# A two-level Strassen MLP: the output bias, S1's sums, A12's own sums and two sets of weight sums put elsewhere

## The chip, the cores and the metric

The kernel runs on one core of a Trainium2 chip. A core has five engines that run their own instruction streams: TensorE (PE; its weight loads are listed as PEld) multiplies matrices, VectorE (DVE), ScalarE (ACT) and GpSimd (POOL) work element by element, and SyncE (SP) issues the DMA transfers here. They are held together by semaphores. Each engine takes its instructions in program order, so an instruction that waits holds up everything behind it on that engine. The metric is the device time of one execution in microseconds; the median of three runs is compared.

## The reference

A cross-attention block and an MLP in float32, with 8 batches of 256 query tokens and 256 context tokens, a model width of 512 and an inner width of 2048. Cut to what matters here:

```python
hidden = cproj(attention(layer_norm(x), ctx)) + x
y = layer_norm(hidden, ln2_w, ln2_b)
y = gelu(y @ fc_w + fc_b, approximate=True)
y = y @ proj_w + proj_b
return hidden + y
```

The change lies in the last three lines, the MLP.

## The kernel before

**Stages.** The first part (to about 350 us) computes the attention for all four groups of 512 tokens and leaves `hidden` in DRAM. The MLP then runs group after group, g = 0 to 3. For each group the first product of the MLP (`fc`, 512 to 2048) comes first, then gelu, then the second product (`proj`, 2048 to 512).

**Strassen's method in Winograd's form.** A product of two matrices, each cut in 2 x 2 blocks, is made of seven block products instead of eight, with sums of blocks taken beforehand and sums of the results afterwards. The blocks of the left matrix A are summed to S1, S2, S3, S4, those of the right matrix B to T1, T2, T4, and the seven products are A11 B11, A12 B21, S2 T2, S3 B12, S1 T1, S4 B22 and A22 T4. In the kernel the sums of A are named `s1` to `s4` and those of B `t1`, `t2`, `t4`. The tables `A_SUMS` and `B_SUMS` hold the four sums of each side.

**`fc`.** `product(k, ...)`, k = 0 to 6, is one of the seven products, and is itself cut into seven by `sub`. One `sub` has eight matmul records. Its results go to PSUM banks (tile `pf`), and VectorE adds them into `u` and then into `h` or `hs`; where a product counts in several blocks of the result, GpSimd adds `hs` into the others (`made`, on GpSimd at line 1122 as `h<-h,hs`). Banks 6 and 7 are single, banks 1 and 5 double. At its end `product` calls `load_w2`, which puts the load of a later product's weights into the ring place just read. The lists `gelus` and `norm` hold work of ScalarE and VectorE that `product` hands out.

**`proj`.** The sums S3 and S2 of the gelu's output are made first (`sum_h`; on VectorE in groups 1 to 3, which are called deep; on GpSimd in group 0), each in four pieces. Here `bias_ht` is called: it adds the output's bias to two quarters of the output tile `ht` (named `resm`), two GpSimd instructions. Then `proj` multiplies A11 by B11 and S3 by B12 whole. In the deep groups the products A12 B21, S2 T2, S1 T1 and S4 B22 are each cut into seven once more by `deep_proj`, which needs the left operand's own sums (`h_blocks`, four sums on VectorE) and the right operand's. VectorE adds each partial product from its bank into a scratch (`p<-pd,p`) and into the result. The instructions handed to `deep_proj` as `others` are put between these adds, in VectorE's order. A12's own sums go to the four quarters of `h["s3"]` (tile `hs`, `free(i)`), which the product S3 B12 still reads; its first two are made before `deep_proj`, the other two and the four sums of S1 are given as `others`. The last of these products, A22 T4, is again whole and accumulates into bank 7.

**Sums of the `proj` weights.** The right operands' own sums are made once by `p2_sums` (four sums of 128x512, then a store of 768 KB to DRAM on SP's queue), in a tile `p2` (shown as `p`) that has two places: `t2` and `22` share the first, `t1` and `21` the second. `t1`'s are made at the end of group 0. Those of `22` and `21` are made on GpSimd when group 1 begins, those of `t2` on VectorE, one in each of group 1's products 3 to 6. Later uses reload them with `p2_load`.

**The end of a group.** `turn_next` transposes the next group's input on TensorE, `sum_up` and `split_y` make its sums on VectorE (`y<-y`), and the last eviction of bank 7 (`o_add` at the very end of the group's loop, `resm<-py,resm`) is behind them in VectorE's order. Group 3 has no next group.

The order is written out by hand: the pools reuse tiles with waits, and there is no scheduler.

Of the kernel before, what the change touches and what calls it, by code (L numbers as in the profile page):

```python
# [22 lines left out]
def tile_xattn_block(  # L23
# [52 lines left out]
    NG = B // GB  # L76
# [9 lines left out]
    HI, HC, HF, HD2 = INNER // 2, NC // 2, NF // 2, D // 2  # L86
# [57 lines left out]
    def place(name, at):  # L144

        return Operand(wts.tile([P, 7, HC, S], F32, tag=f"w{at}", name=name))
# [23 lines left out]
    def rows_of(t):  # L170
        return t.rearrange("p i h s -> p i (h s)")
# [13 lines left out]
    w2, w2_place = {}, {}  # L185
# [137 lines left out]
    with ExitStack() as att:  # L323
# [460 lines left out]
        V, GP = nc.vector, nc.gpsimd  # L784
# [175 lines left out]
        g = 1  # L960
        begin(g, 6, 1, load_res, 0, *QUARTERS)
        begin(g, 7, 1, bias_res, 0)
        g = 2
# [6 lines left out]
        g = NG - 1  # L970
# [24 lines left out]
        def run(pieces):  # L995
            for p in pieces:
                p()
# [18 lines left out]
        t = work.tile([P, NHG, G], F32, tag="att", name="w2_b")  # L1016
# [84 lines left out]
    with ExitStack() as mlp:  # L1101
# [8 lines left out]
        NQF = HF // 2  # L1110
# [59 lines left out]
        def p2_sums(n, eng=V):  # L1170
            x = pw_blocks(n)
            for i in range(4):
                sum_up(eng, x, B_SUMS, i)
                if i == 3:
                    nc.sync.dma_start(p2_dram[n], p2_place(n))
                yield

        p2_t2 = p2_sums("t2")

        def p2_load(n):  # L1180
            nc.sync.dma_start(p2_place(n), p2_dram[n])
# [8 lines left out]
        for g in range(NG):  # L1190
# [18 lines left out]
            def sum_h(which, q, eng=GP):  # L1209

                x = {n: h[n][:, :, 2 * q : 2 * q + 2, :] for n in h}
                to, a, b, op = {
                    "s3": ("s3", "11", "21", ALU.subtract),
                    "s2": ("21", "22", "s3", ALU.subtract),
                    "s1": ("11", "21", "11", ALU.add),
                    "s4": ("12", "12", "21", ALU.subtract),
                }[which]
                add(eng, x[to], x[a], x[b], op)
# [21 lines left out]
            def bias_ht():  # L1240

                for b, bias in ((0, projb[:, :HD2]), (1, pbd)):
                    o = out_quarter(b, 0)
                    add(GP, o, o, by_tiles(bias))
# [8 lines left out]
            def gelu(n, half):  # L1253
                def one(p):
                    nc.scalar.activation(  # L1255
                        h[n][:, :, p, :],
                        h[n][:, :, p, :],
                        AF.Gelu_apprx_tanh,
                        bias=col(c_fcb, half * HF + p),
                        scale=1.0,  # L1260
                    )

                gelus.extend(lambda p=p: one(p) for p in range(HF))
# [5 lines left out]
            def product(k, *sums):  # L1269


                wt, yn = w2[g, k], QI[FC_ORDER[k][1]]
                bank = {}

                def y_of(n):
                    if n in QUARTERS:
                        return ys[g].t[:, yn, int(n[0]) - 1, ts(int(n[1]) - 1, P)]
                    return y2s[g][:, ("t1", "t2", "t4").index(n), yn, :]

                def sub(n, w, b, first, last):  # L1280
                    if first:
                        bank[n] = bank_of(n, f"pf{n}_{k}").rearrange("p i (j s) -> p (i j) s", j=2)
                    for m in range(HF // 2):
                        mm(
                            bank[n][:, m, :],
                            wt[:, QI[w], ts(m, P)],
                            y_of(b),
                            first and m == 0,
                            last,
                        )  # L1290

                def u(n):
                    return us(n, f"u{n}_{k}").rearrange("p i (j s) -> p (i j) s", j=2)

                def made(cd, n, x):
                    some_gelus()
                    if k in (3, 4) and cd != "22":
                        norm_piece()
                    if sums[0][1] is None:
                        add(V, block(sums[0][0], cd), bank[n], x)  # L1300
                        return

                    r = h["s3"][:, parts[0] % 4 // 2, parts[0] % 2 * HF // 2 :][:, : HF // 2]
                    parts[0] += 1
                    add(V, r, bank[n], x)
                    for to, base in sums:
                        add(GP, block(to, cd), block(base, cd), r)

                sub(1, "11", "11", True, False)
                u1 = u(1)  # L1310
                nc.scalar.copy(u1, bank[1])  # L1311
                if g == 1 and k > 2:
                    next(p2_t2)
                sub(6, "s2", "t2", True, True)
                u2 = u(2)
                add(V, u2, bank[6], u1)
                some_gelus()
                sub(7, "s3", "12", True, False)
                u3 = u(3)
                add(V, u3, bank[7], u2)  # L1320
                some_gelus()
                sub(5, "21", "t1", True, False)
                made("22", 5, u3)
                sub(1, "12", "21", False, True)
                some_gelus()
                for to, base in sums:
                    if base:
                        add(V, block(to, "11"), bank[1], block(base, "11"))
                    else:
                        nc.scalar.copy(block(to, "11"), bank[1])  # L1330
                sub(7, "22", "t4", False, True)
                made("21", 7, u2)
                sub(5, "s4", "22", False, True)
                made("12", 5, u2)
                load_w2(w2_place[g, k])


            if g == 1:
                for n in ("22", "21"):
                    for _ in p2_sums(n, GP):  # L1340
                        pass
            product(0, ("21", None))
            load_next()
            product(1, ("11", "21"))
            gelu("11", 0)
            ht = residual(work, hid_dram[g], "resm", f"resm_{g}")
            product(2, ("21", "21"))
            product(3, ("12", "21"))
            if g == 0:
                load_pw("11", "12", "22")  # L1350
# [15 lines left out]
            for which in ("s3", "s2"):  # L1366
                for q in range(NQF):
                    sum_h(which, q, V if deep else GP)
            bias_ht()

            bank = {n: bank_of(n, f"py{n}") for n in ((1, 7) if deep else (1, 7, 6, 5))}

# [20 lines left out]
            def turn_next(c):  # L1393
                if g + 1 < NG:
                    ps = ps_m.tile([P, G], F32, tag="mm", name=f"pyt_{g + 1}_{c}")
                    turn_hid(ps, g + 1, c)

            def o_add(eng, b, k, x):
                o = out_quarter(b, k)
                add(eng, o, x, o)  # L1400
# [13 lines left out]
            def free(i):  # L1414

                return h["s3"][:, i // 2, i % 2 * HF // 2 :][:, : HF // 2]

            def h_blocks(n, s3, s2, s4, s1=None):


                x = {
                    f"{i + 1}{k + 1}": h[n][:, i, k * HF // 2 : (k + 1) * HF // 2, :]
                    for i in range(2)
                    for k in range(2)
                }
                x |= {"s3": s3, "s2": s2, "s4": s4, "s1": x["21"] if s1 is None else s1}

                def one(to, a, b, op):
                    add(V, x["s1" if to == "21" else to], x[a], x[b], op)

                return x, [lambda t=t: one(*t) for t in A_SUMS]
# [33 lines left out]
            def as_tiles(r):  # L1465

                return r.rearrange("p c s -> p (c s)").rearrange("p (i s) -> p i s", i=2)

            if deep:
                x_s2, pieces = h_blocks("21", *(hsum[:, i] for i in range(4)))  # L1470
                run(pieces)
                s1_sums = [lambda q=q: sum_h("s1", q, V) for q in range(NQF)]
            else:
                for q in range(NQF):
                    sum_h("s1", q)
            proj(bank[7], "s3", "12", True, False)
            turn_next(0)
            turn_next(1)
            some_pw(4)
            if deep:  # L1480
                x_12, pieces = h_blocks("12", *(free(i) for i in range(4)))
                run(pieces[:2])
                deep_proj(
                    x_12, "21", hsum[:, 4], pieces[2:3], pieces[3:], s1_sums[:1], s1_sums[1:3], s1_sums[3:]
                )
                p2_load("t1")
                x_s1, s1_own = h_blocks("11", free(0), free(1), free(2))
                run(s1_own[:2])
            else:
                proj(bank[1], "12", "21", False, True)  # L1490
                o_add(V, 0, 0, bank[1])
            for q in range(NQF):
                sum_h("s4", q)
            if deep:
                o_add(GP, 0, 0, as_tiles(hsum[:, 4]))
            turn_next(2)
            turn_next(3)
            some_pw(4)
# [103 lines left out]
```

## Time and profile before

| what | value |
|---|---|
| median of 3 runs | 733.42 us (729.81 to 734.86) |
| the profiled execution | 734.46 us |
| its span | 732.70 us |
| mean granted TensorE clock | 0.998 |
| DMA over the span | 149.90 MB, 205 GB/s mean |
| group 0's MLP, `fc` and `proj` | 350.4 to 444.7 us |
| group 1 | 444.7 to 541.5 us |
| group 2 | 541.5 to 634.8 us |
| group 3 | 634.8 to the end |

The profile is one execution. A row of the timeline has the start and the duration in us, the engine, the line, the operation, what it writes and reads, the shape, and how many instructions were merged; in brackets is the idle time before it and whose end it waited for. A row of the list of waits has the total, the number and the longest. Helpers such as `add` (line 1122) and `sum_up` (line 219) record every operation under their own line, so tiles tell more than lines. The ends of matmuls are modelled, so rows of TensorE overlap a little; starts are used for differences.

### The profile page before, as it was taken

The page shows a single profiled execution, that of the slowest core. Times are in us where ns is not written, and L with a number is a line of the kernel's source. Part 1 is how long each engine was busy: PE and PEld are TensorE (multiplying, and loading weights), DVE is VectorE, ACT ScalarE, POOL GpSimd, SP SyncE. Part 2 cuts the span into 40 slices and gives each one's busy share as a digit, 9 for nine tenths or more (in the row PEclk, how much of TensorE's full clock was granted, in tenths as well). Part 3 has the DMA queues.
Part 4 walks back from the last instruction along what each step waited for, and adds up shares of the span by engine and source line. Part 5 has one row for each costly group of instructions (what it writes and reads, how often), then busy time and mean ns, then how long its engine had stood idle before and what let it go on. Part 6 is the DMA issues. An engine that isn't in the chain of part 4 may idle for free.

```text
span 732.7 us, 14870 instructions
## 1 busy us (share of the span) xinstructions
PE 717.7 (98%) x5397; PEld 633.8 (87%) x5397; DVE 514.7 (70%) x1200; ACT 327.9 (45%) x928; POOL 501.5 (68%) x434
## 2 busy tenths in 40 slices
PE   8999999999999999999999998999999999999988
PEld 7888777887888778777999888999999989999887
DVE  2676755675557557879588597888877888766881
ACT  2268688767777778871226200235112251022400
POOL 3758699987786999876569974693435834447343
PEclk9999999999999999999999999999999999999999
DMA  9515646688648776932899315983339822383021
GB/s 300 169 67 171 246 160 224 201 303 274 201 145 294 269 257 214 350 103 87 296 405 370 136 44 185 397 290 136 130 114 399 301 107 99 132 332 129 1 87 58
DMA packets 77401, 149.90 MB, mean 205 GB/s; under 512 B 7140, under 2 KB 45328, under 8 KB 74640
## 3 DMA queue, kind: packets, MB, share of 16 engines
q1 hardware_dynamic: 77072, 148.92, 57.8%
q8 instruction: 43, 0.70, 0.4%
q14 instruction: 30, 0.25, 0.1%
q0 software_dynamic: 256, 0.02, 0.0%
HBM read 112.22 MB, written 36.70 MB: 203 GB/s over the span
## 4 chain that ended last, share of the span: by engine, by line
PE 84%; DVE 9%; issue 3%; ACT 1%; POOL 1%; DMA 1%; SPq 0%; DVEq 0%; ACTq 0%; POOLq 0%
PE pf L1119 21%; PE py L1119 9%; PE ppt L699 8%; PE pv L441 7%; PE pqT L441 7%; PE po L441 6%; PE pkT L441 5%; PE s L646 5%; PE av L715 4%; PE pd L1119 4%; PE pd_t L1119 4%; PE pkT L538 2%; DVE h L1122 2%; DVE hs L1122 2%; PE pxt L274 1%
## 5 line engine op out<-in xcount | busy, mean ns | idle before, releaser
L1119 PE MATMUL pf<-y,w 128*128 128x128 f32 x1568 | 176.3, 275 | 2.8 <-DVE resm L1122 2.6
L1119 PEld LDWEIGHTS pf<-y,w 128*128 128x128 f32 x1568 | 175.9, 192 | 3.4 <-DVE resm L1122 2.8
L1122 POOL TENSOR_TENSOR h<-h,hs 128x512 f32<-128x512 f32 x88 | 113.4, 1310 | 78.0 <-DVE hs L1122 77.2
L688 POOL TENSOR_TENSOR pr<-pr,rsum 128x512 f32<-128x512 f32 x128 | 129.6, 1045 | 36.4 <-DVE rsum L686 24.0
L674 ACT ACTIVATE pr<-pr,nmax 128x256 f32<-128x256 f32 x256 | 127.7, 502 | 35.5 <-DVE nmax L664 35.3
L664 DVE CUSTOM_DVE_ANT_0 pr<-s,mb 128x256 f32<-128x256 f32 x256 | 93.6, 414 | 40.2 <-PE s L646 30.0
L1311 ACT COPY u<-pf 128x512 f32<-128x512 f32 x28 | 16.4, 586 | 164.2 <-PE pf L1119 164.2
L699 PEld LDWEIGHTS ppt<-ident,pr 128*128 128x128 f32 x512 | 57.3, 140 | 14.9 <-issue 5.9
L699 PE MATMUL ppt<-ident,pr 128*128 128x128 f32 x512 | 68.8, 276 | 0.3
L1122 DVE TENSOR_TENSOR hs<-pf,u 128x512 f32<-128x512 f32 x72 | 49.5, 688 | 13.2 <-PE pf L1119 12.1
L1255 ACT ACTIVATE h<-h,cols 128x256 f32<-128x256 f32 x128 | 52.0, 494 | 11.2 <-POOL h L1122 11.2
L1122 DVE TENSOR_TENSOR u<-pf,u 128x512 f32<-128x512 f32 x56 | 38.7, 691 | 25.8 <-PE pf L1119 22.0
L1122 POOL TENSOR_TENSOR h<-h,h 128x512 f32<-128x512 f32 x20 | 32.1, 1637 | 34.3 <-DVE hs L1122 34.3
L704 ACT COPY pt<-ppt 128x512 f32<-128x512 f32 x96 | 51.8, 574 | 7.1 <-PE ppt L699 7.1
L441 PE MATMUL pv<-vw,ctxT 128*128 128x256 f32 x224 | 52.4, 380 | 0.0
L441 PE MATMUL pqT<-xnT,qw 128*128 128x256 f32 x224 | 51.0, 379 | 0.0
L674 ACT ACTIVATION_READ_ACCUMULATOR pr<-pr,nmax 128x1 f32 x256 | 48.9, 191 | 0.0
L441 PEld LDWEIGHTS pqT<-xnT,qw 128*128 128x128 f32 x224 | 41.4, 190 | 5.0
L441 PEld LDWEIGHTS pv<-vw,ctxT 128*128 128x128 f32 x224 | 41.0, 190 | 5.4 <-ACT xnT L415 0.3
L1119 PE MATMUL py<-pw,h 128*128 128x256 f32 x192 | 42.4, 379 | 0.0
L1119 PE MATMUL py<-pw_t,h 128*128 128x256 f32 x192 | 42.3, 379 | 0.0
L1119 PEld LDWEIGHTS py<-pw_t,h 128*128 128x128 f32 x192 | 36.2, 190 | 4.8
(202 smaller groups left out, 1320.7 us busy)
## 6 DMA issues: line engine op xcount, KB each, us to landing
w<-w_dram SPq DMA_DIRECT2D x16, 1792.0 KB, 9.5
w<-in_L_xattn_fc_w_dram SPq DMA_DIRECT2D x36, 256.0 KB, 5.7
w<-w_dram SPq DMA_DIRECT2D x12, 768.0 KB, 7.3
ctx<-in_ctx_dram SPq DMA_DIRECT2D x16, 256.0 KB, 4.7
x<-in_x_dram SPq DMA_DIRECT2D x16, 256.0 KB, 4.0
v_dram<-st_v SPq DMA_DIRECT2D x16, 256.0 KB, 2.2
v<-v_dram SPq DMA_DIRECT2D x16, 256.0 KB, 4.6
resx<-in_x_dram SPq DMA_DIRECT2D x16, 256.0 KB, 4.8
```

The source lines that it names most:

```text
L441: nc.tensor.matmul(bank[n][:, i, :], l[:, c, ts(i, P)], r[:, c, :], start=first and i == 0 and c == 0, stop=last and c == HC - 1, skip_gro ...
L646: nc.tensor.matmul(banks[j][:, i, :], qT[j * HD : (j + 1) * HD, b * S + i * P : b * S + (i + 1) * P], kT[j * HD : (j + 1) * HD, b * SK : ( ...
L664: nc.vector.tensor_tensor_reduce(pr[:, j, i, :], banks[j][:, i, :], mbias[g][1][:, b, :], scale=-SCALE, scalar=FLT_MAX, op0=ALU.add, op1=A ...
L674: nc.scalar.activation(pr[:, j, i, :], pr[:, j, i, :], AF.Exp, bias=nmax[:, j, i : i + 1], scale=-1.0, accum_out=sums[:, j, i : i + 1],)
L688: nc.gpsimd.tensor_tensor(pr[:, j], pr[:, j], rsum[:, j, :, None].to_broadcast([P, NQ, SK]), ALU.mult,)
L699: nc.tensor.transpose(ps[:, kc, ts(i, P)], probs[n][:, j, i, ts(kc, P)], ident)
L704: nc.scalar.copy(pt, ps)
L715: nc.tensor.matmul(av[j * HD : (j + 1) * HD, :], vs[g, hg][:, b * NK + kc, ts(j, HD)], pts[n, j][:, kc, :], start=(kc == 0), stop=(kc == N ...
L1119: nc.tensor.matmul(ps, lhsT, rhs, start=first, stop=last, skip_group_check=True)
L1122: eng.tensor_tensor(to, a, b, op)
L1255: nc.scalar.activation(h[n][:, :, p, :], h[n][:, :, p, :], AF.Gelu_apprx_tanh, bias=col(c_fcb, half * HF + p), scale=1.0,)
L1311: nc.scalar.copy(u1, bank[1])
```

## The change

Four things are moved; no arithmetic is added or left out.

- `bias_ht` in the deep groups is called after S4's sums and the first output add on GpSimd, and no longer behind the S2 sums.
- S1's four sums (on VectorE in deep groups) come ahead of the product S3 B12 in program order, and so ahead of A12's own sums; these are made in one block before `deep_proj`, which gets no `others`. In group 3 they go to a ring place of the weights (that of product 4, `h_own`) instead of `h["s3"]`.
- `22`'s weight sums go from GpSimd to VectorE: two in group 1's product 0, one each in products 1 and 2. `t2`'s go to products 4, 5 and 6 (one, one, two).
- `21`'s weight sums stay on GpSimd, two behind product 1 and two behind product 2. The stores of `22` and `21` move with them on SP's queue.

```diff
-        p2_t2 = p2_sums("t2")
+        p2_late = {n: p2_sums(n, e) for n, e in (("22", V), ("21", GP), ("t2", V))}
+
+        def some_p2(n, pieces):
+            for _ in zip(range(pieces), p2_late[n]):
+                pass
...
                 nc.scalar.copy(u1, bank[1])
-                if g == 1 and k > 2:
-                    next(p2_t2)
+                if g == 1:
+
+                    some_p2("22", (2, 1, 1, 0, 0, 0, 0)[k])
+                    some_p2("t2", (0, 0, 0, 0, 1, 1, 2)[k])
                 sub(6, "s2", "t2", True, True)
...
-            if g == 1:
-                for n in ("22", "21"):
-                    for _ in p2_sums(n, GP):
-                        pass
             product(0, ("21", None))
             load_next()
             product(1, ("11", "21"))
+            if g == 1:
+                some_p2("21", 2)
             gelu("11", 0)
             ht = residual(work, hid_dram[g], "resm", f"resm_{g}")
             product(2, ("21", "21"))
+            if g == 1:
+                some_p2("21", 2)
...
-            bias_ht()
+            if not deep:
+                bias_ht()
...
-                s1_sums = [lambda q=q: sum_h("s1", q, V) for q in range(NQF)]
-            else:
-                for q in range(NQF):
-                    sum_h("s1", q)
+            for q in range(NQF):
+                sum_h("s1", q, V if deep else GP)
             proj(bank[7], "s3", "12", True, False)
...
             if deep:
-                x_12, pieces = h_blocks("12", *(free(i) for i in range(4)))
-                run(pieces[:2])
-                deep_proj(
-                    x_12, "21", hsum[:, 4], pieces[2:3], pieces[3:], s1_sums[:1], s1_sums[1:3], s1_sums[3:]
-                )
+                own = [free(i) for i in range(4)]
+                if g + 1 == NG:
+
+                    t = rows_of(place("h12_own", w2_place[g, 4]).t)
+                    own = [t[:, i].rearrange("p (c s) -> p c s", c=HF // 2) for i in range(4)]
+                x_12, pieces = h_blocks("12", *own)
+                run(pieces)
+                deep_proj(x_12, "21", hsum[:, 4])
...
             if deep:
                 o_add(GP, 0, 0, as_tiles(hsum[:, 4]))
+                bias_ht()
```

## The prediction

> **What bounds the kernel now.** The page first: TensorE is busy for 98% of the span, and the chain of waits lies on it for 84%, on VectorE for 9%. So nothing gains unless it closes a gap of TensorE. The list of waits for TensorE from 440 us to the end names the gaps; then the timelines around each.
>
> ```profile
> PE 717.7 (98%) x5397; PEld 633.8 (87%) x5397; DVE 514.7 (70%) x1200; ACT 327.9 (45%) x928; POOL 501.5 (68%) x434
> ...
> PE 84%; DVE 9%; issue 3%; ACT 1%; POOL 1%; DMA 1%; SPq 0%; DVEq 0%; ACTq 0%; POOLq 0%
> ...
> PE pd_t L1119 <- DVE p L1122: 4.8, 3, 2.2
> PE pf L1119 <- DVE resm L1122: 2.6, 1, 2.6
> PE pd L1119 <- DVE hs L1122: 0.7, 3, 0.2
> ```
>
> Three stalls on `p` and three on `hs`, one of each per deep group (1, 2, 3), and one on `resm` where group 1 begins. All wait for VectorE. Why VectorE is late, at group 1's start (timeline; columns are start and duration):
>
> ```profile
> 445.45 2.11 POOL L219 TENSOR_TENSOR p<-pw,p 128x512 f32<-128x512 f32 x1
> ...
> 446.36 2.15 DVE L307 TENSOR_TENSOR y<-y,y 128x896 f32<-128x896 f32 x1
> 448.43 0.68 DVE L1122 TENSOR_TENSOR resm<-py,resm 128x512 f32<-128x512 f32 x1
> ...
> 449.16 3.06 PE L1119 MATMUL pf<-y,w 128*128 128x128 f32 x25 [2.57 <-DVE resm L1122]
> ```
>
> TensorE had ended its sixteen matmuls at 446.60; the eviction `resm` that frees bank 7 stands in VectorE's order behind the `y` blocks, and these take 2.15 us beside GpSimd's `p` sums, but 1.08 us each at 539 and 540 us with GpSimd idle. The second place, in group 2:
>
> ```profile
> 586.53 5.70 DVE L1122 TENSOR_TENSOR hs<-h,h 128x512 f32<-128x512 f32 x4
> 592.16 2.49 DVE L1122 TENSOR_TENSOR h<-h,hs 128x512 f32<-128x512 f32 x4
> ...
> 602.88 6.83 POOL L1122 TENSOR_TENSOR h<-h,h 128x512 f32<-128x512 f32 x4 [11.80 <-DVE hs L1122]
> ...
> 608.70 1.55 DVE L1122 TENSOR_TENSOR h<-h,h 128x512 f32<-128x512 f32 x1
> 610.18 1.75 DVE L1122 TENSOR_TENSOR hs<-h 128x512 f32<-128x512 f32 x1
> ...
> 613.31 1.16 PE L1119 MATMUL pd_t<-p,h 128*128 128x128 f32 x8 [1.30 <-DVE p L1122]
> ```
>
> One SBUF sum costs VectorE 0.62 us alone (2.49 / 4), about 1.7 beside GpSimd, which itself goes from 1.27 to 1.71 (6.83 / 4). S1's sums (`h<-h,h`) and S1's own blocks (`hs<-h`) run beside GpSimd's S4 sums, so the add into `p` comes late and TensorE, wanting that bank back, stops.
>
> **What can be won.** A deep stretch is 28 partial products of 0.893 us (521.89 to 528.14 us holds seven), 25.0 us when fed. Group 1 takes 506.47 to 534.39 less 0.87 of transposes, 27.05; group 2 599.76 to 627.70 less 0.87, 27.07; group 3 692.20 to 722.07, 29.87. Lost: 2.05, 2.07, 4.87. With 2.56 at 446.60 that is 11.55 us.
>
> Of group 3's loss 1.55 us isn't idle time: sixteen matmuls from 707.03 to 710.37 take 3.34 us instead of 1.79, at half clock:
>
> ```profile
> 707.00:708.00 1.00, 1.00 (x7) 1.00 (x7) 0.77 (x3) 0.00 (x0) 0.00 (x0) 0.56 0.00 0
> 708.00:709.00 1.00, 1.00 (x7) 1.00 (x6) 0.22 (x2) 0.00 (x0) 0.00 (x0) 0.50 0.81 184
> ```
>
> (behind the stretch's length and five busy times stands the granted clock). This follows a gap of 2.3 us. The Trainium skill, "TensorE: Matmul & The Clock Gate", Part 1, says that the clock drops only after an idle window of about 3.4 us, running freely. By that rule a 2.3 us gap could not do it, the drop would have another cause and stay, and the most to win would be 10.0. But the drop comes only here, right behind the longest gap after two shorter ones; the 2.56 us gap at 446.60 left the clock at 1.00. I take 11.55 and keep 10.0 for the range.
>
> **Part 1, bias behind S4.** Per deep group two GpSimd adds (1.72 us beside VectorE) leave the time of the S3 sums and come behind S4's sums and the first output add. The four S3 sums then meet only the end of GpSimd's last h adds: 5.70 becomes one of 1.5 and three of 0.62, 3.4; VectorE gains 2.3. The price: GpSimd, idle after the output add for 10.7 us (until `resm<-hs` at 622.09), now runs 3.4 us there, beside S1's own s1 and s4 blocks: 1 us dearer each on VectorE. The later output adds on GpSimd keep 7.3 us of idle time in front of them. No DMA moves.
>
> **Part 2, S1's sums and A12's own block.** The four S1 sums cost 5.1 us now (0.98 + 2.56 + 1.55), and move to where GpSimd is idle: 2.5. They overwrite the operand of the product before; the add before them has waited for that product. Group 2, worked from its rows: S3 sums end 589.9, S2 sums 592.4, two evictions 593.6, four own blocks 596.2 (2.65, as at 595.77), S1 598.7, then A12's own s3 599.4, s2 600.1, s1 600.8, s4 601.4. TensorE starts the deep stretch at 599.76 and wants s2 at 600.66, s3 at 601.55, s1 at 602.44: all there, the least margin 0.5. The 0.42 us stall on `hs` goes. With the adds of the product no longer queued behind sums, S1's own s3 and s2 run at 606.3 to 609.7, the `p` adds at 609.9 and 610.1 against a need at 611.4: the 1.47 us stall goes. Group 1's rows give the same margins but 0.3 for s2. In group 3, which has no transposes, s1 and s4 would wait for the S3 product to leave `hs`; the ring place, free since product 4, takes that wait away and costs no instruction or DMA; s2 comes at 693.1 against 693.09, a stall of 0 to 0.2.
>
> What is late next: the third product's add, behind S1's s1 and s4 and two output sums. Group 2: s1 done 612.6, s4 614.3, sums 615.8, S4's own s3 and s2 617.3, add 617.5; need 617.6. In group 3, where each product starts without the 0.87 of cover, it is 709.9 against 709.2. I charge 0.7 there and 0.15 in groups 1 and 2 each: 1.0.
>
> **Part 3, the weight sums.** Eight GpSimd sums (1.60 to 2.11 us, 429.48 to 447.56 with waits) leave group 1's start. VectorE's `y` sums fall from 4.83 to 2.6 and the `y` blocks from 7.9 to 4.3, so they end near 443, before TensorE leaves `py` at 444.65; the eviction is then done at 445.5, and the 2.56 goes. B22's four sums join VectorE: two in product 0 and one each in 1 and 2, where it idles 1.16 us before each first add (row at 455.79); two behind the eviction end at 446.8, the second partial product at 446.4, so its add is 0.3 late and the 0.9 us of the next one covers it. With the cover gone they would cost 2.5. t2 loses its place in product 3 and has two in product 6, where GpSimd is busy (477.73 to 494.89): 2 x 1.15 by the `p` row at 486.41 against 0.69 before, 0 to 0.5 on TensorE; taken 0.3. B21's four come to 5.1 to 6.8 us on GpSimd in products 1 to 3, which has idle gaps of 2.0, 0.6, 1.5, 1.0, 0.4 and 1.6 us there; it catches up before the run that starts at 477.73.
>
> DMA (times from here as they would be with the 2.56 us gone): the two 768 KB stores move in SP's queue behind the loads of weights 3 and 4 and of `resm`, in front of weights 5 and 6. B22's waits for its last sum at about 459, so it doesn't hold weight 5 (free at 463.8); B21's waits for GpSimd until about 472 and holds weight 6, free at 469.7, by 2 to 3 us. It lands in 5 to 7 us, 480, against a need at 482. Bytes are unchanged (transfers take 9 to 12 us with the engines full from 450 to 478). t2's first sum overwrites B22's sums, so it waits for their store: issued 459, landed by 471.4 at the worst shown (12.4 us), wanted at 470.4, and the adds behind it have 1 us of room. Cost 0, bounded by 0 and 2.
>
> **The sum.** 11.55 - 1.0 - 0.3 = 10.25. The profiled execution took 734.46 us (span 732.70 and 1.76 around it): 724.2. It is 1.04 above the median of 733.42, so on the median 723.2.
>
> **Rivals.**
> A, half of it comes back, 21%: GpSimd now runs from S4's sums through the bias without a pause, and the stall on `p` moves to the third product in each group. For it: margins of 0.1 us and the 1.7 us that each sum takes there. Against: three of those sums are off the path. At 1.5 us a group beyond what is charged, 10.25 - 4.5 = 5.75 remains: 733.4 - 5.75 = 727.7.
> B, it doesn't do what it says, 9%: the S3 sums are set by the gelu and by GpSimd's last h adds, not by the bias, so the deep stretches keep their gaps and only group 1's start is won. For it: ScalarE runs its 24 gelus until 592.2 in group 2. Against: S3 needs only the first eight. 2.6 us remains: 730.8.
> C, slower, 4%: VectorE halts in product 4 on B22's store. Place: t2's first sum, in front of that product's adds, with both banks and TensorE behind. It costs 1 us for each us past 471.4, and outweighs the gain only if the store lands after 483, that is 24 us after its issue; the longest transfer shown is 12.4. At 28 us it gives 738.
>
> **How the numbers follow.** The main case has 66%, own range 720 to 726.5 (10.0 instead of 11.55, the charges between 0 and 3, and medians of three that scatter by some 2 us). The 8-in-10 range is 720 to 730, which takes in A. One per cent of 733.4 is 7.3 us, about what a measurement of this kernel tells from no change: faster than 726.1 holds most of the main case and a little of A, 0.64; within it 0.32; slower by more 0.04.
>
> **What would show it.** Right: no TensorE gap at group 1's start, the `y` blocks at 1.08 us, deep stretches of 25 to 26 us without transposes, granted clock 1.00 throughout, S3's sums in about 3.4 us. Wrong: a wait of `pd_t` for `p` in the third deep product; VectorE waiting for a DMA at t2's first sum; weight 6 late.

## The result, and the profile after

| | before | after |
|---|---|---|
| median (range, runs) | 732.66 us (729.81 to 734.86, 4) | 722.62 us (722.45 to 723.32, 4) |
| profiled execution, its span | 734.46, 732.70 us | 723.32, 721.5 us |

The ratio is 0.9867 (95% interval 0.9831 to 0.9903): faster by 1.3%, 0.6 us from the predicted 723.2. (A fourth run of before has joined the three whose median was 733.42.) The runs of after also lie closer together, within 0.9 us instead of 5.

The page of after first, the line of busy times and the chain that ended last:

```profile
PE 712.7 (99%) x5397; PEld 630.9 (87%) x5397; DVE 504.9 (70%) x1204; ACT 327.8 (45%) x928; POOL 486.1 (67%) x430
...
PE 87%; DVE 3%; DMA 2%; ACT 2%; POOL 2%; issue 2%; SPq 0%; DVEq 0%; ACTq 0%; POOLq 0%
```

TensorE's share of the chain rose from 84 to 87%, VectorE's fell from 9 to 3%. The list of TensorE's waits from 430 us on (total, times, longest):

```profile
PE pf L1119 <- DVE u L1122: 1.5, 3, 0.7
PE pd L1119 <- DVE h_own L1122: 0.3, 1, 0.3
```

The three waits that the prediction set out to close, on `p`, `hs` and `resm`, are gone. Two are left: on `u`, now 1.5 us in three places, and a new one on `h_own`. Before, `u` had one wait of 0.3 us, a row that the prediction leaves out of its list:

```profile
PE pf L1119 <- DVE u L1122: 0.3, 1, 0.3
```

**Group 1's start**, in the timeline of after. First VectorE:

```profile
440.01 1.08 DVE L307 TENSOR_TENSOR y<-y,y 128x896 f32<-128x896 f32 x1
443.25 0.69 DVE L1122 TENSOR_TENSOR resm<-py,resm 128x512 f32<-128x512 f32 x1 [2.15 <-PE py L1119]
```

The `y` blocks cost 1.08 us each with GpSimd silent, against up to 2.15 before. They are done before bank 7 is, so the eviction now waits for TensorE and no longer the other way round.

**Products 4 to 6 of group 1**, the same timeline, TensorE and then VectorE:

```profile
442.98 29.64 PE L1119 MATMUL pf<-y,w 128*128 128x128 f32 x264
473.31 6.52 PE L1119 MATMUL pf<-y,w 128*128 128x128 f32 x56 [0.70 <-DVE u L1122]
480.14 6.52 PE L1119 MATMUL pf<-y,w 128*128 128x128 f32 x56 [0.31 <-DVE u L1122]
487.18 2.05 PE L1119 MATMUL pf<-y,w 128*128 128x128 f32 x16 [0.52 <-DVE u L1122]
```

```profile
470.25 1.61 DVE L219 TENSOR_TENSOR p<-pw_t 128x512 f32<-128x512 f32 x1 [0.35 <-DMA p_dram<-p]
471.79 1.47 DVE L1122 TENSOR_TENSOR u<-pf,u 128x512 f32<-128x512 f32 x2
...
482.91 1.15 DVE L219 TENSOR_TENSOR pw_t<-pw_t 128x512 f32<-128x512 f32 x1
483.98 1.75 DVE L219 TENSOR_TENSOR p<-pw_t,p 128x512 f32<-128x512 f32 x1
```

No gap of TensorE at 446 us any more, but three small ones later. The first comes behind `t2`'s first sum: it waits 0.35 us for B22's store (issued at 457.40), then takes 1.61 us beside a run of GpSimd, and the two adds into `u`, which free the banks, stand behind it. The second is what is left of that lateness one product on. The third comes behind the pair of `t2`'s sums in product 6, 2.90 us together.

**Group 2's deep stretch**, VectorE and then GpSimd:

```profile
581.79 3.55 DVE L1122 TENSOR_TENSOR hs<-h,h 128x512 f32<-128x512 f32 x4
...
591.51 2.49 DVE L1122 TENSOR_TENSOR h<-h,h 128x512 f32<-128x512 f32 x4
...
603.31 1.65 DVE L1122 TENSOR_TENSOR hs<-h,hs 128x512 f32<-128x512 f32 x1
604.88 0.68 DVE L1122 TENSOR_TENSOR p<-pd_t,p 128x128 f32<-128x128 f32 x2
...
606.18 1.69 DVE L1122 TENSOR_TENSOR h<-hs,h 128x512 f32<-128x512 f32 x1
...
611.73 0.28 DVE L1122 TENSOR_TENSOR p<-pd_t,p 128x128 f32<-128x128 f32 x1
```

```profile
600.23 2.50 POOL L1122 TENSOR_TENSOR h<-h,h 128x512 f32<-128x512 f32 x2 [1.05 <-ACT hsum L1464]
...
604.49 1.60 POOL L1122 TENSOR_TENSOR resm<-resm,projb 128x512 f32<-128x512 f32 x1
606.05 1.27 POOL L1122 TENSOR_TENSOR resm<-resm,pbd 128x512 f32<-128x512 f32 x1
```

S3's sums went from 5.70 to 3.55 us and S1's from 5.1 to 2.49. The adds into `p` at 604.88 are in time, and so is the third product's at 611.73. The bias (604.49 to 607.32) makes one of S1's own blocks dearer (606.18, 1.69 us) where two were charged, with no stall behind it.

**Group 3.** VectorE, then TensorE:

```profile
685.97 0.69 DVE L1122 TENSOR_TENSOR h_own<-h,h_own 128x512 f32<-128x512 f32 x1
```

```profile
685.40 1.05 PE L1119 MATMUL pd<-pw,h 128*128 128x128 f32 x8
686.71 1.16 PE L1119 MATMUL pd<-p,h_own 128*128 128x128 f32 x8 [0.26 <-DVE h_own L1122]
```

A12's own s2 ends at 686.66; TensorE would have begun on it at 685.40 + 0.89 = 686.29 and begins at 686.71, 0.42 us late. The granted clock stays at 1.00 throughout this stretch.

By stretches of TensorE (starts of the first matmuls; groups 1 and 2 with their 0.87 us of transposes): the deep ones take 25.89, 25.89 and 25.53 us against 27.92, 27.94 and 29.87 before, 2.03, 2.05 and 4.34 won. Group 1's `fc` (first `pf` to first `py`) takes 46.09 against 47.13, 1.04 won. That is 9.46 us. A further 1.7 us of the 11.2 us between the two spans is at the very start, among the first loads: the first row of 24 `pkT` matmuls (line 538) begins at 15.18 us in before and at 13.52 in after. The change touches nothing there, and in the eight experiments the same row stands at 12.26 to 13.18; it is not counted as a gain.

### The profile page after: what moved, and what is told of

Same layout as the page of the kernel before. It is cut to its first block, busy times and chain, and to the rows that moved or that the text cites. A ratio compares the mean times of both kernels' runs of the same rounds, so it can differ in the third digit from the quotient of the medians.

```text
span 721.5 us, 14867 instructions
## 1 busy us (share of the span) xinstructions
PE 712.7 (99%) x5397; PEld 630.9 (87%) x5397; DVE 504.9 (70%) x1204; ACT 327.8 (45%) x928; POOL 486.1 (67%) x430
## 4 chain that ended last, share of the span: by engine, by line
PE 87%; DVE 3%; DMA 2%; ACT 2%; POOL 2%; issue 2%; SPq 0%; DVEq 0%; ACTq 0%; POOLq 0%
PE pf L1119 18%; PE py L1119 12%; PE ppt L699 8%; PE pv L441 7%; PE pqT L441 7%; PE po L441 6%; PE pd_t L1119 5%; PE pd L1119 5%; PE pkT L441 5%; PE s L646 5%; PE av L715 5%; PE pkT L538 2%; POOL h L1122 2%; ACT h L1259 2%; DMA pw<-in_L_xattn_proj_w_dram 2%
## 5 line engine op out<-in xcount | busy, mean ns | idle before, releaser
L1122 POOL TENSOR_TENSOR h<-h,h 128x512 f32<-128x512 f32 x20 | 27.5, 1398 | 42.9 <-DVE hs L1122 13.4
```

What stands on the lines that cost most here:

```text
L1122: eng.tensor_tensor(to, a, b, op)
```

## The experiments

Two questions. Which of the three parts brings the gain, and do they need each other? And what are the `u` stalls of group 1, which the prediction put at 0.3 us? My theory of the first: bias and S1's order each serve only together, since each alone moves VectorE's dear sums beside GpSimd's work. The rivals: the order of S1's sums is enough; or the bias is. Four runs shared 19 runs of before (median 732.71, 729.99 to 734.33): the bias early, S1's sums as they were, the weight sums back, and no ring place. The other four shared 7 (733.09, 731.38 to 733.82). Edits are against the changed kernel unless said otherwise.

### The bias early again

```diff
-            if not deep:
-                bias_ht()
+            bias_ht()
...
                 o_add(GP, 0, 0, as_tiles(hsum[:, 4]))
-                bias_ht()
```

> The changed kernel with the bias put back ahead of S4 (behind the S2 sums in the program, on GpSimd); all else as changed. Theory (GpSimd's two bias adds slow the S3 sums, and everything in front of the deep product is one line of VectorE work without slack): S3's four sums take 5.7 us again instead of 3.55, A12's own s2 comes 2.1 us later, and TensorE waits for it about 1.7 us at the second partial product in groups 1 and 2 and 2.6 in group 3 (now 0, 0 and 0.42): about 5.5 us more than the changed kernel, 728. If the S3 sums were bound by the gelu, they would stay near 3.6 us and the time at 722.6.

Measured: 730.13 us (728.62 to 731.36, 10 runs), ratio to before 0.9972 (0.9956 to 0.9987); 7.5 us above the changed kernel, where I had told 5.5. Its list of waits and, in its timeline, group 2's S3 sums and the stall:

```profile
PE pd L1119 <- DVE hs L1122: 3.4, 2, 1.8
PE pd L1119 <- DVE h_own L1122: 2.4, 1, 2.4
```

```profile
584.11 5.71 DVE L1122 TENSOR_TENSOR hs<-h,h 128x512 f32<-128x512 f32 x4
```

```profile
599.96 1.16 PE L1119 MATMUL pd<-p,hs 128*128 128x128 f32 x8 [1.56 <-DVE hs L1122]
```

S3's sums are back at 5.71 us, and with S1's 2.49 us now ahead of A12's own, s2 comes 1.56 to 2.41 us late in all three groups. So S1's new place, with the bias early, takes the wait away from `p` and puts it on A12's own sums (`hs`, in group 3 `h_own`). The deep stretches of this profile are 6.05 us longer than those of the changed kernel (27.96, 27.71 and 27.69 us), near the 5.5 told; a further 1.3 us lies between the first loads and group 1's `fc`, where the edit changes nothing.

### S1's sums and A12's own as they were

```diff
-            for q in range(NQF):
-                sum_h("s1", q, V if deep else GP)
+                s1_sums = [lambda q=q: sum_h("s1", q, V) for q in range(NQF)]
+            else:
+                for q in range(NQF):
+                    sum_h("s1", q)
...
-                own = [free(i) for i in range(4)]
-                if g + 1 == NG:
-
-                    t = rows_of(place("h12_own", w2_place[g, 4]).t)
-                    own = [t[:, i].rearrange("p (c s) -> p c s", c=HF // 2) for i in range(4)]
-                x_12, pieces = h_blocks("12", *own)
-                run(pieces)
-                deep_proj(x_12, "21", hsum[:, 4])
+                x_12, pieces = h_blocks("12", *(free(i) for i in range(4)))
+                run(pieces[:2])
+                deep_proj(
+                    x_12, "21", hsum[:, 4], pieces[2:3], pieces[3:], s1_sums[:1], s1_sums[1:3], s1_sums[3:]
+                )
```

> The changed kernel with S1's sums and A12's last two own sums put back between the adds of the first deep product, and A12's own sums back in the gelu's S3 tile; bias and weight sums as changed. Theory (S1's sums and S1's own blocks beside GpSimd's S4 sums make the stalls; the bias's place alone gives nothing, since VectorE then only idles earlier): the waits of TensorE for p and hs are back, about 2.0 us in groups 1 and 2 and 4.9 in group 3 with half clock behind the long gap: 722.6 + 8.5 = 731. Rival, the faster S3 sums alone give the gain: 723 to 725.

Measured: 735.53 us (732.94 to 737.87, 10 runs), ratio 1.0041 (1.0021 to 1.006), 4.5 above what I expected, and slower than before although S3's sums and group 1's start are mended. The waits, and group 2's VectorE, GpSimd and TensorE:

```profile
PE pd_t L1119 <- DVE p L1122: 7.6, 3, 3.1
```

```profile
609.85 1.63 DVE L1122 TENSOR_TENSOR hs<-h,hs 128x512 f32<-128x512 f32 x1
611.41 0.67 DVE L1122 TENSOR_TENSOR p<-pd_t,p 128x128 f32<-128x128 f32 x2
```

```profile
609.35 1.59 POOL L1122 TENSOR_TENSOR resm<-resm,projb 128x512 f32<-128x512 f32 x1
```

```profile
612.13 1.20 PE L1119 MATMUL pd_t<-p,h 128*128 128x128 f32 x8 [2.23 <-DVE p L1122]
```

The bias in its new place stands beside S1's own s2, which takes 1.63 us where the kernel before, with GpSimd done, has 0.69; the add into `p` is behind it, and the stall grows from 4.8 to 7.6 us. I had expected the old stall there, not a larger one: the move of the bias has its own price whenever S1's sums are late.

### The bias alone

The same, without the weight sums: before, with nothing but the bias moved (`bias_ht()` behind `o_add`, as in the change).

> The kernel before with the bias moved behind S4's sums and nothing else. Theory from the run with own sums split: the S3 sums get faster but the adds of the first deep product still wait for TensorE, so VectorE only idles longer in front of them, and the bias on GpSimd now slows S1's own s2 (1.63 instead of 0.69 us), the last sum before the add into p: TensorE's three waits for p grow from 4.8 to about 7.6 us, and a longer gap halves the clock more often: 3 to 5 us more than before, about 736.5. Rival, the bias alone is a gain: 730 or less.

Measured: 737.14 us (736.52 to 739.34, 4 runs), ratio 1.0065 (1.0042 to 1.0087). In its timeline S3's sums are as fast as in the changed kernel, and the stall is there:

```profile
587.70 3.55 DVE L1122 TENSOR_TENSOR hs<-h,h 128x512 f32<-128x512 f32 x4
...
613.13 1.63 DVE L1122 TENSOR_TENSOR hs<-h,hs 128x512 f32<-128x512 f32 x1
```

That separates the two rivals: 2.15 us won on S3's sums are worth nothing, since these had room (in group 2 VectorE's idle time before the first add into `p` grows from 1.90 to 4.05 us, by just as much), and the end of the chain, S1's own s2 and the `p` add, became later. The waits on `p` are 7.6 us instead of 4.8, and this profile has three stretches at half clock where the one of before has one. Part 1 pays only where part 2 has pulled that end of the chain forward.

### The weight sums back at group 1's start

```diff
-                    some_p2("22", (2, 1, 1, 0, 0, 0, 0)[k])
-                    some_p2("t2", (0, 0, 0, 0, 1, 1, 2)[k])
+                if g == 1 and k > 2:
+                    some_p2("t2", 1)
...
+                for n in ("22", "21"):
+                    for _ in p2_sums(n, GP):
+                        pass
             product(0, ("21", None))
```

> The changed kernel with the weight sums of 22 and 21 back on GpSimd at group 1's start and t2's back in products 3 to 6; the rest as changed. Theory: the wait for the eviction at group 1's start is back (2.56 us), the three waits on u in products 4 to 6 of group 1 go from 1.52 to 0.26: 1.3 us more, 723.9. If the weight sums were worth their whole 2.56, 725.2; if nothing, 722.6.

Measured: 724.09 us (723.64 to 725.63, 4 runs), ratio 0.989 (0.9859 to 0.992). The `u` wait is back at its 0.3 us, and TensorE waits at group 1's start:

```profile
446.58 8.64 PE L1119 MATMUL pf<-y,w 128*128 128x128 f32 x75 [2.58 <-DVE resm L1122]
```

So part 3 is worth 1.5 us by the medians and 1.05 by the length of group 1's `fc` (47.14 us here, 46.09 in the changed kernel), not 2.26: of the 2.56 won, 1.1 to 1.5 was lost again in products 4 to 6.

The parts against before, by the medians: part 1 alone +4.0 us, parts 1 and 3 +2.8, parts 2 and 3 -2.6, parts 1 and 2 -8.6, all three -10.0. Part 2 or part 3 alone was not run. Parts 2 and 3 still gain without part 1, though hardly more than the 1.0 to 1.5 us of part 3. So the theory holds for the bias, which alone is a loss; that S1's order alone gains nothing is not shown.

### Without the ring place

```diff
                 own = [free(i) for i in range(4)]
-                if g + 1 == NG:
-
-                    t = rows_of(place("h12_own", w2_place[g, 4]).t)
-                    own = [t[:, i].rearrange("p (c s) -> p c s", c=HF // 2) for i in range(4)]
```

> The changed kernel with A12's own sums of group 3 in the gelu's S3 tile as in groups 1 and 2, instead of the ring place of the weights. What the prediction said: s1 and s4 would wait there for the product that reads the tile, 0.5 to 1 us on TensorE. Theory from the trace: that product ends at 685.40 and VectorE reaches s1 only at 686.69, so there is nothing to wait for: no difference, 722.6.

Measured: 722.2 us (722.11 to 722.26, 4 runs), ratio 0.986 (0.9826 to 0.9894). Group 3, VectorE and TensorE:

```profile
685.56 0.69 DVE L1122 TENSOR_TENSOR hs<-hs,h 128x512 f32<-128x512 f32 x1
686.17 0.69 DVE L1122 TENSOR_TENSOR hs<-h,hs 128x512 f32<-128x512 f32 x1
```

```profile
684.17 1.05 PE L1119 MATMUL pd<-pw,h 128*128 128x128 f32 x8
685.51 1.16 PE L1119 MATMUL pd<-p,hs 128*128 128x128 f32 x8 [0.28 <-DVE hs L1122]
```

s1 and s4 (the two rows of VectorE) write the tile that S3's product read, without a wait: that product has left it by 684.17 and s1 comes only at 685.56. The ring place takes away a wait that isn't there, to which the prediction had given no size. And this kernel's trace lacks the stalls of products 4 and 5, in group 1, which the edit doesn't touch: B22's store took 12.6 us here and 12.8 in the changed kernel, so `t2`'s first sum finds it landed and costs 0.69 us instead of 1.61. VectorE's and GpSimd's row, and behind them GpSimd's of the changed kernel:

```profile
469.94 0.69 DVE L219 TENSOR_TENSOR p<-pw_t 128x512 f32<-128x512 f32 x1
```

```profile
467.13 4.64 POOL L1122 TENSOR_TENSOR h<-h,hs 128x512 f32<-128x512 f32 x3
```

```profile
467.22 4.09 POOL L1122 TENSOR_TENSOR h<-h,hs 128x512 f32<-128x512 f32 x3
```

GpSimd is at work beside it in both. The Trainium skill, "SBUF — State Buffer", "SBUF: two separate sides", says that VectorE (with two operands from SBUF) and GpSimd take their shared port for a whole instruction, and that whoever comes second waits. The two traces fit that: here GpSimd's three sums took 4.64 us, in the changed kernel 4.09, while VectorE's sum took 0.69 and 1.61. VectorE's sum begins 2.81 us into GpSimd's row here and 3.03 there: in these two traces 0.2 us decides which of the two pays. Group 1's `fc` takes 44.96 us here against 46.09, so 1.13 us hang on that sum.

### `t2`'s first sum one product earlier

```diff
-                    some_p2("t2", (0, 0, 0, 0, 1, 1, 2)[k])
+                    some_p2("t2", (0, 0, 0, 1, 1, 1, 1)[k])
```

> The changed kernel with t2's weight sums in products 3, 4, 5 and 6, one each, as the kernel before had them, while 22's stay in products 0 to 2. Theory (t2 overwrites the place from which 22's store still reads): VectorE reaches t2's first sum at about 463 and waits for the store, which landed at 470.2 in the changed kernel's trace: some 7 us, of which TensorE loses 5 to 6; product 6 has one sum less, which gives back 0.5: about 727.5. If the store's landing is no bound, 722.1.

Measured: 729.0 us (728.35 to 729.87, 4 runs), ratio 0.9945 (0.9926 to 0.9965). VectorE's row, TensorE's, and two stretches of the granted clock:

```profile
469.93 0.69 DVE L219 TENSOR_TENSOR p<-pw_t 128x512 f32<-128x512 f32 x1 [7.64 <-DMA p_dram<-p]
```

```profile
472.08 8.20 PE L1119 MATMUL pf<-y,w 128*128 128x128 f32 x49 [6.11 <-DVE u L1122]
```

```profile
471.00:472.00 1.00, 0.00 (x0) 0.00 (x0) 0.90 (x2) 0.00 (x0) 0.00 (x0) 0.50 0.93 395
...
474.00:475.00 1.00, 1.00 (x6) 1.00 (x6) 0.97 (x4) 0.00 (x0) 0.26 (x1) 0.50 0.19 80
```

VectorE halts for 7.64 us on B22's store, which was issued at 457.00 and takes until 469.9; the two banks stay full and TensorE stops 6.11 us, then runs its first 49 matmuls in 8.20 us at half clock where 5.5 is usual. This is rival C's mechanism: one product earlier it costs 6.4 us.

### The store early, and then A12's own s3 and s2 first

If the store and the pair of sums make the stalls, a kernel that issues the store earlier and never has two sums in a row late should have none. B22's first two sums go ahead of group 0's last eviction, the other two into product 0, and `t2`'s into products 1, 2, 5 and 6:

```diff
-                    some_p2("22", (2, 1, 1, 0, 0, 0, 0)[k])
-                    some_p2("t2", (0, 0, 0, 0, 1, 1, 2)[k])
+                    some_p2("22", (2, 0, 0, 0, 0, 0, 0)[k])
+                    some_p2("t2", (0, 1, 1, 0, 0, 1, 1)[k])
...
                 split_y(g + 1, y2, 0, 1, 2, 3)
+                if g == 0:
+                    some_p2("22", 2)
                 proj(bank[7], "22", "t4", False, True)
```

> The changed kernel with 22's first two sums in front of the last eviction of group 0, where VectorE idles 2.15 us, the other two in product 0, and t2's in products 1, 2, 5 and 6, one each. Theory: the store is issued about 12 us earlier with the DMA engines idle, t2 meets no wait, and products 3 and 4, which carry the next group's norm, get no sum; TensorE's three waits on u in group 1 (1.52 us) fall to 0.3 or less: 721.3. If the eviction is delayed by the two sums in front of it, a wait of TensorE on it comes back.

Measured: 720.95 us (720.35 to 721.41, 4 runs), ratio 0.9838 (0.9821 to 0.9855). The store leaves at 444.06, 13.3 us earlier than in the changed kernel, and lands in 3.4 us; `t2`'s first sum overwrites its tile without a wait:

```profile
448.93 0.68 DVE L219 TENSOR_TENSOR p<-pw_t 128x512 f32<-128x512 f32 x1
```

The wait on `u` is gone; the list of waits from 430 us on has one row left, `h_own` with 0.3 us. Group 1's `fc` takes 43.97 us (441.87 to 485.84) instead of 46.09.

The second step, on top: A12's own s3 and s2 ahead of S1's sums, s1 and s4 behind them.

```diff
-            for q in range(NQF):
-                sum_h("s1", q, V if deep else GP)
+            else:
+                for q in range(NQF):
+                    sum_h("s1", q)
...
-                run(pieces)
+                run(pieces[:2])
+                for q in range(NQF):
+                    sum_h("s1", q, V)
+                run(pieces[2:])
```

> The same as the run with the early store, and A12's own s3 and s2 made in front of S1's four sums, its s1 and s4 behind them. Theory: s2 is ready 2.4 us earlier, so group 3's wait of TensorE for it (0.42 us with the gap's loss) goes and nothing later is late, since s1 is wanted only two partial products on: 0.4 less than that run, 720.9. Rival: s1 comes too late in one of the groups, and the wait moves to the fourth partial product: no gain.

Measured: 719.97 us (719.72 to 720.38, 4 runs), ratio 0.9826 (0.981 to 0.9842). Group 3's VectorE and TensorE:

```profile
680.67 0.69 DVE L1122 TENSOR_TENSOR h_own<-h,h_own 128x512 f32<-128x512 f32 x1
681.28 2.49 DVE L1122 TENSOR_TENSOR h<-h,h 128x512 f32<-128x512 f32 x4
683.69 0.68 DVE L1122 TENSOR_TENSOR h_own<-h_own,h 128x512 f32<-128x512 f32 x1
```

```profile
682.51 1.05 PE L1119 MATMUL pd<-pw,h 128*128 128x128 f32 x8
683.41 1.06 PE L1119 MATMUL pd<-p,h_own 128*128 128x128 f32 x8
```

s2 is ready 2 us before it is wanted; from 430 us on the list of TensorE's waits is empty, and group 3's stretch takes 25.02 us, the fed length, 0.51 less than with the early store alone. I had told 0.4; the medians differ by 0.98, and the ranges just touch (720.38 and 720.35). Against the changed kernel it is 2.65 us by the medians; the two were not run side by side, so that figure is the looser one.

## Why the prediction was right, and where its terms were not

- **"What can be won", 11.55 us.** Right: the gaps counted are the gaps that closed. The half clock behind group 3's gap, which I took at 1.55 us against the rule that I weighed, did go with the gap: of the 4.87 us that group 3's deep stretch had lost, 4.34 came back. That it stood in the one profile read was the common case and not a sure one (last section).
- **Part 1.** Durations right (3.4 us told, 3.55 measured; one of S1's own blocks 1 us dearer). What the text didn't say is that this part alone makes the kernel slower: 4.0 us over before. There the bias meets S1's own s2; without part 2, part 1 is a loss.
- **Part 2.** Right in groups 1 and 2: every own block is in time. Two errors in group 3. "A stall of 0 to 0.2" for s2 was 0.42. And "takes that wait away", said of the ring place, was wrong: without it there is no wait either.
- **"What is late next", 1.0 us.** Mis-sized: it is nothing. Carried to the stretch of after, which starts at 595.01 instead of 599.76, my add, done at 617.5, would be done at 612.75; it was done at 612.01, against a need at about 612.9, and in group 3 at 702.59 against 702.89. I had charged both S1's s1 and s4 with 1.7 us beside GpSimd. But in group 2 the bias ended at 607.32, and s4, at 607.99, cost 0.67. GpSimd was early because S4's sums, which in before wait for A12's own sums, began 1.38 us into the stretch (596.39) instead of 3.12 (602.88), and the last two took 2.50 us instead of 3.4. So part 2 pulls GpSimd forward as well, which the prediction leaves out.
- **Part 3, 2.56 less 0.3.** The gap of 2.56 went by the mechanism given. The term that failed is the loss in the later products, charged at 0.3: of the 2.56 only 1.04 remains in the length of `fc`, so 1.5 was lost. Without the ring place, where `t2`'s first sum met no late store, `fc` is 2.17 shorter than before, so the loss is 0.4: the pair in product 6 was charged about rightly, and the other 1.1 hangs on `t2`'s first sum. Its wait for B22's store was put at "Cost 0, bounded by 0 and 2", with an issue at 459, a landing by 471.4 and a want at 470.4. The store was issued at 457.40, took 12.8 us and ended 0.35 us after the want. What I left out is that the sum behind the wait can be the dear one: it took 1.61 us instead of 0.69.
- **The sum.** 10.25 told, 9.46 in the stretches of the profile, 10.04 between the medians. By term, 1.0 was lost less (third product), 0.5 more (group 3) and 1.2 more (products 4 to 6): they cancel in part, and the nearness of 723.2 to 722.6 is to that extent luck.
- **The rivals.** A (the stall moves to the third product) did not happen. B is excluded by S3's sums at 3.55 us and by the run with the bias early. C's mechanism is real, with 0.35 us of wait here and 7.64 us one product earlier; of the three signs of being wrong that were named, VectorE's wait for a DMA at `t2`'s first sum is the one that appeared.

## What to carry to other kernels

Where two engines slow each other, a move pays only if it leaves the last operation before the bound engine's wait alone: find that operation first (here the second own block and the add into `p`), since a sum made faster elsewhere on the same engine bought nothing and cost 4 us. Parts of one reordering are therefore tried together and undone one by one. A sum that overwrites what a store still reads is priced by the store's landing, not by its own duration, and the landing is not a constant: the same 768 KB took 12.9 us behind the loads of weights and of `resm`, and 3.4 us when issued before them.

## What the hardware showed that was not expected

A gap's length alone did not decide whether the clock dropped. In the run with S1's sums as before, TensorE stops for 2.23 us in groups 1 and 2 and for 3.10 us in group 3, with a drop only in group 2. Its stretches behind the gap in group 2, and behind the one in group 3 (stretch, then five busy times, then the granted clock):

```profile
613.00:614.00 1.00, 1.00 (x8) 1.00 (x7) 0.78 (x3) 0.00 (x0) 0.00 (x0) 0.56 0.03 8
614.00:615.00 1.00, 1.00 (x6) 1.00 (x6) 0.26 (x1) 0.00 (x0) 0.00 (x0) 0.50 0.49 74
...
708.00:709.00 1.00, 1.00 (x11) 1.00 (x10) 0.82 (x3) 0.00 (x0) 0.00 (x0) 1.00 0.00 0
```

With the bias alone the same gaps dropped it in groups 1 and 2 and again not after the 3.10; there the gap of 2.56 us at group 1's start dropped it too, which in before and with the weight sums back there (2.57 and 2.58 us) left it at 1.00. So gaps of 2.2 us can cost half clock, against the idle window of about 3.4 us of the Trainium skill ("TensorE: Matmul & The Clock Gate", Part 1), and need not; what decides was not tried. It goes with the spread: of the kernels with such gaps, before differs by 4.3 us over its 19 runs and the one with S1's sums as before by 4.9 over 10, while the changed kernel and the last two differ by about 1 over 4. And the times of the 19 runs of before follow their mean clock: 729.99 to 730.92 us at 1.0 (four runs), 731.45 to 733.43 at 0.997 and 0.998 (eight), 732.93 to 734.33 at 0.994 and 0.995 (seven); its profile, with one stretch at half clock, has 0.998. So some executions of before have no drop, and against the four at 1.0 the changed kernel gains 7.7 us by the medians and not 10.
